# The first sequence's convolutions between the steps of the step-length preparation (layer 0 of a four-layer network)

## The chip, the cores and the metric

The kernel runs on one core of a Trainium2 chip. The metric is the time of one launch on the device, in microseconds (us), as the median of several runs; lower is better. One execution was taken with the hardware profiler. The engines are PE (matrix products), DVE (vector), ACT (scalar functions), POOL (general purpose), and SP, which issues most of the transfers. They run independently of each other, each takes its own instructions strictly in order, and they wait for each other through semaphores.

## The reference

Four layers work on four sequences of 512 tokens with 256 features, in float32. Each layer normalizes its input and adds the results of a mixer and of a feed-forward part, both from the same normalized input. The change concerns layer 0, whose mixer is a Mamba-2 state space model and whose feed-forward part is a gated unit:

```python
    x = L0_attn_hidden_states
    xn = _layernorm(x, axis=-1)
    x = x + _L0_attn_ref(xn, ...) + _L0_ffn_ref(xn, ...)
```

```python
            proj = jnp.einsum('bld,pd->blp', hidden_states, W_in)
            gate = proj[..., :INTER]
            hBC = proj[..., INTER:INTER + CONV_DIM]
            dt = proj[..., INTER + CONV_DIM:]
            xc = jnp.transpose(hBC, (0, 2, 1))
            conv = jax.lax.conv_general_dilated(xc, conv_w[:, None, :], ...)   # 4 taps, causal, per channel
            hBC = _silu(jnp.transpose(conv + conv_b[None, :, None], (0, 2, 1)))
            xs = hBC[..., :INTER].reshape(b, l, H, P)
            Bm = hBC[..., INTER:INTER + G * N].reshape(b, l, G, N)
            Cm = hBC[..., INTER + G * N:].reshape(b, l, G, N)
            ...
            dt = jax.nn.softplus(dt + dt_bias)
            A = -jnp.exp(A_log)
            dA = jnp.exp(dt * A)
            def step(h, inp):
                dA_t, dt_t, x_t, B_t, C_t = inp
                u = (dt_t[:, :, None] * x_t)[..., None] * B_t[:, :, None, :]
                h = dA_t[:, :, None, None] * h + u
                y = jnp.einsum('bhpn,bhn->bhp', h, C_t)
                return (h, y)
            ...
            g = y * _silu(gate)
            g = g * jax.lax.rsqrt(jnp.mean(g * g, axis=-1, keepdims=True) + EPS) * norm_w
            return jnp.einsum('bli,di->bld', g, W_out)
```

There are 32 heads of 64 channels (INTER = 2048), one group of B and C with 128 states, and 4 taps. So three things come out of the input projection: the channels x, B and C, which go through the convolution; the gate; and one step length per token and head, which doesn't. The step lengths dt decide how far each token's state decays.

## The kernel before, in words

Layer 0 runs as two interleaved streams, written as Python generators: `mamba_pieces` (the mixer) and `glu_units` (the gated feed-forward units, and also two sequences of a unit of layer 1). Each stream yields after a small piece of work and says with a number how much that piece is worth. `weave` always continues the stream that has done the smaller share of its announced total, 630.0 for the mixer and 207.0 for the gated units. The yielded numbers thus decide how many gated-unit pieces stand between two mixer pieces in the program. A scheduler then lays the instructions of each engine out in an order near that of the program; it may move an instruction ahead of one that isn't ready by its own reckoning, and it places the waits. It also assigns the buffers: tiles with one tag of one pool share a fixed number of buffers, and a new tile waits until the one before it in the buffer is no longer read. PSUM, where PE writes, has eight banks: four with the tag `mm`, two `tr` and two `acc`.

The mixer runs in this order:

- *The step lengths* (`with tc.tile_pool(name="m_pre", ...)`, lines 276 to 333): PE projects 32 numbers for each of the 2048 tokens into one bank (L142); DVE and ACT compute softplus from exp and a series of seven terms, about twenty DVE operations on 128x512 tiles (z, e, s, w, q; L285 to L305), into `dt`, and `dA`, the logarithm of the decay (L307). For each of the four sequences PE transposes dA (L315) and sums it along the chunk (L316); ACT exponentiates both into `row` tiles (L322), DVE sets the first decay of each chunk to zero (L324), and SP writes them to DRAM as `own` and `since` (L325). Two products (L331) and Exps (L332) give `after` and `etot`. All temporary tiles stand in a pool of their own, m_pre, which is closed behind this; only then are the pools of the rest opened. The piece yields 30, 20, 30, four times 1.5, and 2.
- *A sequence's B and C* (`sequence`): a projection (L134 on `ws`), the first tap on ACT (L264), three taps on DVE (L268) and Silu on ACT (L272) for each, and then transposes of B (L356) and products of B and C for the four chunks (L357, `CB`).
- *A group's channels* (`group(i, k)`, four tiles k for each of 16 groups i, a group being 512 channels, eight heads, of one sequence): projection, convolution to `xc`, and the gate's projection and Silu to `sg` (L388).
- *Chunks* of 128 tokens, 64 of them (16 groups of 4): SP loads the decays `G` from own, spread over 128 partitions (L394), and `eb` from since (L425); DVE turns G into running products with a scan (L409); PE transposes xc (L415), DVE multiplies by dt into `xdt`; POOL multiplies G by CB (L435); PE computes the part from the state (L456), the state's update (L464) and the part within the chunk (L474); y goes through the gate and into the output projection (L495), added on DVE (L501). The next group's tiles are computed within the chunks of the group before it.

The gated units' pieces are two projections (L134 on `wu`), Silu (L195), a product on DVE into `hT` (L196), and then the down projection (L203) with its addition into x (L151).

The first sequence and the first group have no chunk ahead of them to be computed in: `sequence(0)` and `group(0, 0..3)` stand between the step lengths and the first chunk.

Of the kernel before, what the change touches and what calls it, by code (L numbers as in the profile page):

```python
# [15 lines left out]
P = 128  # L16
# [3 lines left out]
TPB = SEQ // P  # L20
# [213 lines left out]
def mamba_pieces(c, a, ws, open_pool):  # L234
# [4 lines left out]
    nc, tc = c.nc, c.tc  # L239
    HG, HD = 8, 64  # L240
    by_head = lambda v: v[:, :, None].to_broadcast([P, HG, HD])
    keep = open_pool("m_keep", 1)
# [6 lines left out]
    wide = [P, NTILE, 32]  # L249
# [23 lines left out]

        return taps

    with tc.tile_pool(name="m_pre", bufs=1, side="right") as pool:

        pd = c.ps()
        for t in range(NTILE):
            project_tokens(  # L280
                c, pd[:, t * 32 : (t + 1) * 32], w_bcd, slice(256, 288),
                slice(t * P, (t + 1) * P),
            )
        z = c.tile(pool, wide, "z")
        nc.vector.tensor_add(z, v3(pd, 32), dt_bias[:, None, :].to_broadcast(wide))  # L285
        e = c.tile(pool, wide, "e")
        nc.vector.scalar_tensor_tensor(e, z, -1.0, z, ALU.mult, ALU.min)
        nc.scalar.activation(e, e, AF.Exp)
        expA = c.tile(pool, [P, 32], "expA")
        tc.keep_in_program_order(nc.scalar.activation(expA, a_log, AF.Exp))  # L290
        yield 30.0
        s = c.tile(pool, wide, "s")
        nc.vector.tensor_scalar_add(s, e, 2.0)
        nc.vector.reciprocal(s, s)
        nc.vector.tensor_mul(s, s, e)
        w = c.tile(pool, wide, "w")
        nc.vector.tensor_mul(w, s, s)
        q = c.tile(pool, wide, "q")
        nc.vector.tensor_scalar_mul(q, w, 1.0 / 17.0)
        yield 20.0  # L300
        for k in range(7, 0, -1):
            nc.vector.scalar_tensor_tensor(q, q, 1.0 / (2 * k + 1), w, ALU.add, ALU.mult)
        nc.vector.scalar_tensor_tensor(q, q, 1.0, s, ALU.add, ALU.mult)
        nc.vector.tensor_scalar_max(z, z, 0.0)
        nc.vector.scalar_tensor_tensor(dt, q, 2.0, z, ALU.mult, ALU.add)  # L305
        dA = c.tile(pool, wide, "dA")
        nc.vector.scalar_tensor_tensor(  # L307
            dA, dt, -1.0, expA[:, None, :].to_broadcast(wide), ALU.mult, ALU.mult
        )
        yield 30.0  # L310
        for b in range(NB):
            pa, pc = c.ps("tr"), c.ps("acc")
            for t in range(TPB):
                cols = slice(t * P, (t + 1) * P)
                nc.tensor.transpose(pa[:32, cols], dA[:, b * TPB + t, :], c.ident)  # L315
                nc.tensor.matmul(  # L316
                    pc[:32, cols], lhsT=dA[:, b * TPB + t, :], rhs=c.le, start=True, stop=True
                )
            tiles = slice(b * TPB, (b + 1) * TPB)
            for src, out in ((pa, own), (pc, since)):  # L320
                row = c.tile(pool, [32, TPB, P], "row", bufs=2)
                nc.scalar.activation(row, v3(src[:32, :], P), AF.Exp)  # L322
                if out is own:
                    nc.vector.memset(row[:, :, 0:1], 0.0)  # L324
                nc.sync.dma_start(out[tiles].rearrange("t h s -> h t s"), row)  # L325
            yield 1.5

        dAf = dA.rearrange("p t h -> p (t h)")
        for tri, out in ((c.gt, after), (c.ones, etot)):
            pc = c.ps()  # L330
            nc.tensor.matmul(pc, lhsT=tri, rhs=dAf, start=True, stop=True)  # L331
            nc.scalar.activation(out.rearrange("p t h -> p (t h)"), pc, AF.Exp)  # L332
        yield 2.0
# [4 lines left out]
    def load_in(i):  # L338
        w_in[i] = c.tile(pg2, [P, 2048], "w_in")
        nc.sync.dma_start(w_in[i], a["m_units"][i % 4][:, :2048])  # L340

    def sequence(b):

        tokens = slice(b * SEQ, (b + 1) * SEQ)
        BT = c.tile(pb, [P, SEQ], "BT", bufs=1)
        CT = c.tile(pb, [P, SEQ], "CT")
        for k, out in ((16, BT), (17, CT)):
            pc = c.ps()
            project(c, pc, w_bcd, slice((k - 16) * P, (k - 15) * P), tokens)
            taps = causal_conv(pool, pc, k, out)  # L350
            yield 1.7
            taps()
        pt, pcb = c.ps("tr"), c.ps("acc")
        for t in range(TPB):
            cols = slice(t * P, (t + 1) * P)
            nc.tensor.transpose(pt[:, cols], BT[:, cols], c.ident)  # L356
            nc.tensor.matmul(pcb[:, cols], lhsT=BT[:, cols], rhs=CT[:, cols], start=True, stop=True)  # L357
        Btok = c.tile(pb, [P, TPB, P], "Btok")
        CB = c.tile(pb, [P, TPB, P], "CB")
        nc.scalar.copy(Btok, v3(pt, P))  # L360
        nc.scalar.copy(CB, v3(pcb, P))
        acc = c.tile(pb, [P, TPB, DM], "acc")
        ssq = c.tile(pb, [P, TPB, 2, P], "ssq", bufs=1)
        seqs[b] = CT, Btok, CB, acc, ssq
        yield 1.3
# [25 lines left out]
    def decays(i, t):  # L391

        G = c.tile(pool, [P, HG, P], "G", bufs=3)
        nc.sync.dma_start(  # L394
            G.rearrange("p h t -> p (h t)"),
            own[i // 4 * TPB + t, i % 4 * HG : (i % 4 + 1) * HG, :]
            .rearrange("h t -> (h t)").partition_broadcast(P),
        )
        Gs[i, t] = G
# [90 lines left out]
    def project_out(i, t, y):  # L490
# [11 lines left out]
        if g == 3 and t == TPB - 1:  # L502
# [11 lines left out]
                add_scaled(c, b * TPB + u, acc[:, u, :], rs[:, u : u + 1])  # L514
            c.part_done(b)

    load_in(0)
    yield from sequence(0)
    for k in range(4):
        taps = group(0, k)  # L520
        yield 3.4
        taps()
    decays(0, 0)
    decays(0, 1)
    before(0, 0)
# [55 lines left out]
def layer0(c, a, x_in, con):  # L581

    with ExitStack() as stack:
        open_pool = lambda name, bufs, **kw: stack.enter_context(
            c.tc.tile_pool(name=name, bufs=bufs, **kw)
        )
        c.weights = open_pool("m_w", 1)
        unit = c.tile(c.weights, [P, 3072], "wu")
        ws = c.tile(open_pool("m_ws", 1), [P, 762], "ws")
        first_loads(c, a, x_in, con, ws, unit)  # L590
        for b in range(NB):
            layernorm(c, b)
            c.step(True)
        glu = open_pool("g0", 1)

        def glu_units():
            same = dict(bufs=5, out_tag="tr")
            yield from glu_pieces(c, glu, [unit], loaded=True, last=False, **same)
            yield from glu_pieces(c, glu, [a["g0_units"][1]], first=1, **same)

            yield from glu_pieces(
                c, glu, [a["g1_units"][0]], last=False, seqs=[0, 1], **same
            )

        c.parts(2, lambda b: layernorm(c, b, c.xn[b * SEQ : (b + 1) * SEQ, :]))
        weave(
            c,
            (mamba_pieces(c, a, ws, open_pool), 630.0, 0.0),
            (glu_units(), 207.0, 0.0),
        )  # L610

# [1169 lines left out]
```

## Time and profile before

| | us |
|---|---|
| median of three runs | 3194.76 (3190.83 to 3198.62) |
| time of the profiled execution | 3179.26 |
| its span | 3177.5 |
| PE busy in it | 3081.6 (97%) |
| DVE / ACT / POOL busy | 1851.9 / 1257.6 / 640.0 |

Layer 0 takes the first 830 us or so of the span; its last output product (L495) ends at 830.3. The tables list for each stage how long each engine was busy, how many of its instructions ran, the clock that PE was granted (1.00 is full) and the transfers. In lists in order of time a line gives the start, the busy time, engine, line, operation, what it writes and reads, how many instructions were merged into it, and in square brackets how long the engine was idle before it and what ended that. PE's matrix instructions appear twice, as the product and as the load of its stationary operand (PEld). One 512-column matmul instruction of the program appears as two in the trace.

### The profile page before, as it was taken

Reading aid. Unit: us, or ns where it says so; the run is one execution under the profiler, and the core shown is the slowest. Engines: PE = TensorE matmul, PEld = TensorE weight load, DVE = VectorE, ACT = ScalarE, POOL = GpSimd, SP = SyncE. Lnnn points to the kernel's source line nnn. Section 1 sums busy time; section 2 is a strip of 40 time slices with the busy share of each in tenths; the row PEclk is TensorE's granted clock in tenths of the full one; section 3 lists DMA queues with packets and bytes.
Section 4 is the critical chain, followed back from the end, with each engine's and each line's share of the span. In section 5 each row is a group of like instructions: output and inputs, shape, how many; then the busy total and the mean of one; then the engine's idle time right before and its main releaser. Section 6 shows DMA issues by size and latency. Waiting matters only on the chain.

```text
span 3177.5 us, 35877 instructions
## 1 busy us (share of the span) xinstructions
PE 3081.6 (97%) x12502; PEld 1879.8 (59%) x12502; DVE 1851.9 (58%) x4786; ACT 1257.6 (40%) x2908; POOL 640.0 (20%) x525
## 2 busy tenths in 40 slices
PE   8999999999899999999989999999999999999999
PEld 5566566565555555555566566566666665555555
DVE  5777778777677777887646654554554522222222
ACT  4434435444356666667424433333333401111111
POOL 0464545555400122331053000000000000000000
PEclk9999999999899999999999999999999999999999
DMA  4233233232310244344143000000000000000000
GB/s 130 77 103 119 93 95 110 89 117 83 110 36 25 68 98 116 103 112 142 47 113 110 7 21 7 1 27 1 21 1 1 20 20 20 20 20 20 0 0 27
DMA packets 89091, 185.16 MB, mean 58 GB/s; under 512 B 14192, under 2 KB 57216, under 8 KB 84176
## 3 DMA queue, kind: packets, MB, share of 16 engines
q1 hardware_dynamic: 74448, 135.05, 13.1%
q0 software_dynamic: 14176, 47.01, 6.1%
q8 instruction: 99, 1.62, 0.2%
q10 hardware_dynamic: 288, 0.82, 0.1%
q14 instruction: 80, 0.66, 0.1%
HBM read 160.95 MB, written 12.98 MB: 55 GB/s over the span
## 4 chain that ended last, share of the span: by engine, by line
PE 78%; DVE 10%; DMA 4%; POOL 3%; ACT 2%; issue 2%; SPq 1%; DVEq 0%; ACTq 0%; POOLq 0%
PE mm L134 31%; PE acc L203 8%; PE mm L631 7%; PE mm L142 5%; PE acc L1102 4%; PE acc L647 3%; DMA G<-own 2%; PE tr L1094 2%; PE tr L495 2%; DVE G L409 2%; DVE cy L268 2%; PE tr L812 2%; PE acc L856 1%; PE acc L869 1%; DMA psw<-pes 1%
## 5 line engine op out<-in xcount | busy, mean ns | idle before, releaser
L134 PE MATMUL mm<-xnT,wu 128*128 128x512 f32 x2128 | 955.6, 596 | 2.3 <-ACT sg L195 0.7
L134 PEld LDWEIGHTS mm<-xnT,wu 128*128 128x128 f32 x2128 | 398.4, 191 | 461.3 <-issue 430.8
L638 ACT ACTIVATE pr<-pr,nm 128x128 f32<-128x128 f32 (+3 forms) x512 | 285.9, 559 | 294.3 <-DVE nm L634 292.8
L195 ACT ACTIVATE sg<-mm 128x512 f32<-128x512 f32 x176 | 104.6, 594 | 607.0 <-PE mm L134 606.9
L196 DVE TENSOR_TENSOR hT<-sg,mm 128x512 f32<-128x512 f32 x176 | 120.4, 684 | 380.7 <-PE mm L134 369.0
L634 DVE CUSTOM_DVE_ANT_0 pr<-mm,late 128x128 f32<-128x128 f32 (+3 forms) x512 | 245.0, 482 | 88.3 <-PE mm L631 82.4
L203 PE MATMUL acc<-wu,hT 128*128 128x256 f32 x1280 | 290.9, 380 | 0.7 <-DVE x L151 0.4
L203 PEld LDWEIGHTS acc<-wu,hT 128*128 128x128 f32 x1280 | 240.0, 190 | 51.3 <-issue 19.2
L134 PE MATMUL mm<-xnT,w_in 128*128 128x512 f32 x512 | 231.1, 596 | 0.4 <-DVE hT L196 0.4
L973 POOL DMA_INDIRECT e<-in_p_experts,ids x128 | 128.4, 1003 | 451.7 <-DVE x L152 366.0
L409 DVE TENSOR_TENSOR_SCAN G<-G,eye 128x1024 f32<-128x1024 f32 x64 | 157.0, 2453 | 52.3 <-DMA G<-own 51.8
L631 PE MATMUL mm<-kf,qf 128*128 128x128 f32 (+3 forms) x512 | 179.1, 446 | 7.9 <-DVE qf L789 5.7
L435 POOL TENSOR_TENSOR G<-G,CB 128x1024 f32<-128x1024 f32 x64 | 151.8, 2372 | 162.0 <-DVE G L409 80.5
L268 DVE SCALAR_TENSOR_TENSOR cy<-mm,ws,cy 128x511 f32<-128x511 f32 (+2 forms) x216 | 158.7, 741 | 41.4 <-ACT cy L264 37.8
L631 PE MATMUL mm<-k,q 128*128 128x128 f32 (+3 forms) x512 | 176.6, 435 | 1.1 <-DVE q L1067 1.1
L421 ACT ACTIVATE xD<-xc,ws 128x128 f32<-128x128 f32 x256 | 84.8, 391 | 203.9 <-POOL y L458 191.6
L134 PEld LDWEIGHTS mm<-xnT,w_in 128*128 128x128 f32 x512 | 97.1, 192 | 101.3 <-issue 94.3
L152 DVE SCALAR_TENSOR_TENSOR x<-acc,cw,x 128x256 f32<-128x256 f32 x128 | 61.9, 483 | 155.5 <-PE acc L203 155.5
L1102 PE MATMUL acc<-PT,V 128*128 128x512 f32 (+3 forms) x512 | 149.5, 433 | 0.0
L1067 DVE TENSOR_SCALAR q<-mm,bias 128x512 f32<-128x512 f32 x64 | 48.0, 750 | 169.1 <-PE mm L134 169.1
L151 DVE TENSOR_TENSOR x<-acc,x 128x256 f32<-128x256 f32 x168 | 70.5, 421 | 118.4 <-PE acc L647 98.4
L812 PEld LDWEIGHTS tr<-con,pr 128*128 128x128 f32 x640 | 81.7, 143 | 90.2 <-ACT pr L805 28.8
(308 smaller groups left out, 5017.8 us busy)
## 6 DMA issues: line engine op xcount, KB each, us to landing
G<-own SPq DMA_DIRECT2D x64, 512.0 KB, 4.3
w_in<-in_m_units SPq DMA_DIRECT2D x16, 1024.0 KB, 5.2
eb<-since SPq DMA_DIRECT2D x96, 128.0 KB, 3.2
wu<-in_o_units SPq DMA_DIRECT2D x8, 1536.0 KB, 6.5
wo<-in_m_units SPq DMA_DIRECT2D x16, 512.0 KB, 3.8
psw<-pes SPq DMA_DIRECT2D x128, 64.0 KB, 2.6
wu<-in_g_units SPq DMA_DIRECT2D x4, 1536.0 KB, 6.8
wu<-in_f_units SPq DMA_DIRECT2D x4, 1536.0 KB, 6.9
```

Of the source, the lines that this page charges most:

```text
L134: c.nc.tensor.matmul(out, lhsT=w[:, d, cols], rhs=c.xnT[:, d, tokens], start=(d == 0), stop=(d == 1))
L142: c.nc.tensor.matmul(out, lhsT=c.xnT[:, d, tokens], rhs=w[:, d, cols], start=(d == 0), stop=(d == 1))
L203: nc.tensor.matmul(po, lhsT=hT[k][:, t * P : (t + 1) * P], rhs=wd[:, k, :], start=(i == 0), stop=(i == per - 1),)
L268: nc.vector.scalar_tensor_tensor(y[:, j:], src[:, : SEQ - j], conv[:, k, 3 - j : 4 - j], y[:, j:], ALU.mult, ALU.add,)
L409: nc.vector.tensor_tensor_scan(flat, flat, eye.rearrange("p h t -> p (h t)"), 0.0, ALU.mult, ALU.add)
L435: nc.gpsimd.tensor_mul(G, G, seqs[b][2][:, t, :][:, None, :].to_broadcast([P, HG, P]))
L631: nc.tensor.matmul(sc, lhsT=q[:, i * P : n], rhs=k[:, :n], start=True, stop=True)
L634: nc.vector.tensor_tensor_reduce(out=pr, in0=sc, in1=late[:, SEQ - n :], scale=1.0, scalar=-NEG, op0=ALU.add, op1=ALU.min, accum_out=nm,)
L638: nc.scalar.activation(pr, pr, AF.Exp, bias=nm, scale=-1.0, accum_out=total)
L812: nc.tensor.transpose(pt[:, (i - j) * P : (i - j + 1) * P], prs[s][i][:, j * P : (j + 1) * P], c.ident)
L973: nc.gpsimd.indirect_dma_start(out=e, out_offset=None, in_=a["p_experts"], in_offset=bass.IndirectOffsetOnAxis(ap=ids[:, t, k : k + 1], ax ...
L1102: nc.tensor.matmul(z[:, j * P :], lhsT=head["V"][:, j, h, :], rhs=head["PT"][:, j, j * P :], start=(j == 0), stop=(j == TPB - 1),)
```

## The change

The preparation of the step lengths becomes a generator, `time_steps`, like the other parts. Its tiles stand in the chunks' pool under the tags S, xw, eb and sq (two buffers each), which the chunks use later for other things; `expA` goes to the pool that stays, and the row tiles are the first 32 partitions of an sq tile. The pool m_pre is gone. The mixer now begins by loading the first group's weights and alternates: step lengths to e and its Exp; projection and first tap of B; the step lengths' s, w and the first q; the other taps of B and the projection of C; the rest of `sequence(0)`; the series, dt and dA; then the first tile of group 0; then the transposes, rows and products of dA; then the other three tiles. The pieces of the preparation yield 6, 4, 6, four times 1.5, and 2, and the mixer's announced total goes from 630 to 566.

```diff
-    with tc.tile_pool(name="m_pre", bufs=1, side="right") as pool:
+    def time_steps():
+
+        wide_tile = lambda tag: c.tile(pool, wide, tag)
...
-        z = c.tile(pool, wide, "z")
+        z, e = wide_tile("S"), wide_tile("S")
         nc.vector.tensor_add(z, v3(pd, 32), dt_bias[:, None, :].to_broadcast(wide))
-        e = c.tile(pool, wide, "e")
         nc.vector.scalar_tensor_tensor(e, z, -1.0, z, ALU.mult, ALU.min)
         nc.scalar.activation(e, e, AF.Exp)
-        expA = c.tile(pool, [P, 32], "expA")
+        expA = c.tile(keep, [P, 32], "expA")
         tc.keep_in_program_order(nc.scalar.activation(expA, a_log, AF.Exp))
-        yield 30.0
-        s = c.tile(pool, wide, "s")
+        yield 6.0
+        s, w, q = wide_tile("xw"), wide_tile("xw"), wide_tile("eb")
...
-        yield 20.0
+        yield 4.0
...
-        dA = c.tile(pool, wide, "dA")
+        dA = wide_tile("eb")
...
-        yield 30.0
+        yield 6.0
...
-                row = c.tile(pool, [32, TPB, P], "row", bufs=2)
+                row = c.tile(pool, [P, TPB, P], "sq")[:32]
...
     load_in(0)
-    yield from sequence(0)
+    steps, first = time_steps(), sequence(0)
+    for stream in (steps, first, steps, first, first, steps):
+        yield next(stream)
+    assert next(first, None) is None
     for k in range(4):
         taps = group(0, k)
         yield 3.4
         taps()
+        if k == 0:
+            yield from steps
...
-            (mamba_pieces(c, a, ws, open_pool), 630.0, 0.0),
+            (mamba_pieces(c, a, ws, open_pool), 566.0, 0.0),
             (glu_units(), 207.0, 0.0),
```

More of the change, by code (lines that the diff above doesn't have):

```diff
@@ L295, in mamba_pieces @@
         nc.vector.tensor_mul(s, s, e)
-        w = c.tile(pool, wide, "w")
         nc.vector.tensor_mul(w, s, s)
-        q = c.tile(pool, wide, "q")
         nc.vector.tensor_scalar_mul(q, w, 1.0 / 17.0)
-        yield 20.0
+        yield 4.0
         for k in range(7, 0, -1):
```

## The prediction

> **What bounds the kernel now.** I read the page's busy table first: PE is busy 3081.6 of 3177.5 us, so time is to be had only where PE waits or is slow. Then the table of stages for the part of layer 0 that the change can reach.
>
> ```profile
> PE 3081.6 (97%) x12502; PEld 1879.8 (59%) x12502; DVE 1851.9 (58%) x4786; ACT 1257.6 (40%) x2908; POOL 640.0 (20%) x525
> ...
> core 0: us, PE busy (x) PEld busy (x) DVE busy (x) ACT busy (x) POOL busy (x), PEclk, DMA share, GB/s
> 30.00:50.00 20.00, 20.00 (x65) 11.72 (x64) 16.92 (x25) 9.94 (x17) 0.00 (x0) 1.00 0.00 0
> 50.00:72.00 22.00, 21.31 (x79) 9.35 (x78) 1.83 (x7) 11.63 (x18) 0.00 (x0) 1.00 0.27 67
> 72.00:105.00 33.00, 29.02 (x91) 14.82 (x91) 27.07 (x32) 16.39 (x31) 8.37 (x5) 0.95 0.24 68
> 105.00:760.00 655.00, 637.94 (x3042) 396.20 (x3039) 512.23 (x661) 289.43 (x602) 349.12 (x236) 1.00 0.31 101
> ```
>
> PE is covered without a gap from 30 to 50 us, although DVE is then computing the step lengths: gate units fill it. DVE is idle from 50 to 72. From 72 to 105 PE loses about 4 us. In the 655 us behind it PE waits 17.1 us, at full clock. Next the order of time at the places that carry the sum:
>
> ```profile
> 30.18 0.69 DVE L285 TENSOR_TENSOR z<-mm,ws 128x512 f32<-128x512 f32 x1 [1.39 <-PE mm L142]
> ...
> 34.55 3.35 DVE L294 RECIPROCAL s<-s 128x512 f32<-128x512 f32 x1
> ...
> 48.10 0.69 DVE L307 SCALAR_TENSOR_TENSOR dA<-dt,expA 128x512 f32<-128x512 f32 x1
> ...
> 49.85 0.27 PE L315 MATMUL tr<-con,dA 128*32 128x128 f32 x1
> ...
> 85.47 4.02 DVE L409 TENSOR_TENSOR_SCAN G<-G,eye 128x1024 f32<-128x1024 f32 x1
> ...
> 91.63 0.33 PE L415 MATMUL tr<-con,xc 128*128 128x128 f32 x1 [2.26 <-ACT xc L272]
> ...
> 93.85 0.47 PE L415 MATMUL tr<-con,xc 128*128 128x128 f32 x1 [1.03 <-ACT xc L272]
> ...
> 104.64 1.09 PE L474 MATMUL acc<-G,xdt 128*64 128x128 f32 x16
> ```
>
> The step lengths are a DVE chain from 30.18 to 48.79. PE waits twice for a convolution's Silu, and behind these waits (94.1 to 97.2) its weight loads come 0.86 us apart instead of 0.43: half speed, 1.6 us lost. 104.64 is the first product with G of chunk 0; I use it as the milestone. Last, PE's waits from 105 to 760:
>
> ```profile
> PE tr L495 <- DVE x L151: 3.3, 3, 1.7
> ...
> PE tr L495 <- DVE acc L501: 2.3, 2, 2.0
> PE tr L356 <- ACT BT L272: 2.3, 2, 1.4
> ```
>
> They are short and scattered; only the third has one fixed place, the turn to a new sequence.
>
> **The change part by part.** Line numbers are those of before. No arithmetic is added or removed: the two built programs hold the same instructions on every engine. PE's order is the same from chunk 62 to the end, and that of the other engines from a little earlier or later, so only about 28 to 780 us can change.
>
> *Gate units leave the preparation.* In before, ahead of the milestone, PE's order holds 32 gate/up matmul instructions and 24 down matmuls (L134 on wu, L203); in after 16 and 12. A 512-column instruction takes 0.86 us (14 passes in 6.17 us), a down matmul 0.45 (16 passes in 3.62 us). So 16 x 0.86 + 12 x 0.45 = 19.2 us of PE work moves behind the milestone. After breaks even if it gets there at 104.64 - 19.2 = 85.4.
>
> *The chain of step lengths gets company on DVE.* Before, three hT products (0.69) and four adds into x (0.42) stood within it; after, three hT and six convolution taps (0.70 each). Its start is 29.4 instead of 30.18, as one gate matmul fewer stands ahead of the last projection. Sum from there: z, e, max 1.8; hT 2.1; the seven q steps 5.0; s and reciprocal 3.8; taps 4.2; s x e, w, q 1.8; last three 2.0; wait for ACT's Exp 0.3. That is 21.0, so dA is ready at 50.4, 1.6 later than before.
>
> *PE runs dry ahead of it.* After the projections end (29.3), PE's new order has eight 512-column tiles of 1.72 (BT's conv projection is done, CT's, two of group 0, five of gate units), four transposes 0.60 and CB 1.05 = 15.4 us, and then L315, which needs dA. So PE is out of work at 44.7 and waits until 50.4: 5.7 us, at a place where before had none. PE's queue is in order, so everything behind L315 waits too.
>
> *The clock behind that wait.* In before, 2.26 and 1.03 us of waiting were followed by 1.6 us lost at half speed, and a 3.72 us wait near the end of the layer (816 us) by rows 0.28, 0.89 and 0.50 longer than elsewhere, together 1.7. I take 1.7.
>
> The Trainium skill, "TensorE: Matmul & The Clock Gate", Part 1, has the clock fall after about 3.4 us of idleness; the 2.26 us wait above did it in this trace already, so the row decides. Its Part 4 says that transposes don't count as busy to the gate, which speaks against this change: the alternating transposes of L315 come right behind the wait. By that rule the 4.4 us of the first eight pairs would all run at half speed and the sum would be 2.7 us higher; the trace only shows that such pairs hold a full clock (50 to 54 us).
>
> *From dA to the milestone.* PE work in the new order: 12 alternating pairs of L315/L316 at 0.55 (their spacing from 50.39 on) = 6.6, the last four grouped 1.65, L331 2 x 0.94, ten 512-column tiles 17.2, twelve down matmuls 5.4, eight xc transposes 1.2, L464 0.95: 34.9. 50.5 + 1.7 + 34.9 = 87.1. Waits in between: the first scan of G (L409) sits on DVE ahead of the taps of group 0's second tile and must wait for its load. own is written at about 54.8, lands 1.7 later, G takes 4.7: DVE gets to the taps at about 65.4, when that tile's projection is only just done (63.6), so this costs PE little. The third scan meets POOL's product and takes 4.02 instead of 2.29, as in before's row; the Exps of the last sequence now stand on ACT, with two table loads of 1.28, between the tiles' Silus. By that walk xc of tiles 2 and 3 comes 1.0 and 1.4 us after PE asks for it: 2.4. Milestone 89.5, against 85.4: **+4.1**. That already counts the waits of before (about 4 us and 1.6) as gone.
>
> *What becomes free of the pool's end.* In before all tiles of the new pools wait for the closed pool: cy, G and others for the eight writes of row, the last issued at 65.90. In after SP issues the first G load behind one own write, and nothing waits for the rest. SP is otherwise waiting, so moving the eight writes among G, eb and w_in loads costs nothing while loads run a chunk ahead; if that cover went, a late G costs up to DVE's longest wait of 3.0. The borrowed buffers cost nothing: S, xw, eb and sq are first wanted by chunks at 82 or later, step lengths are done with them at about 60, the row writes at 76. POOL's queue keeps its order there.
>
> *The steady stage.* 19.2 us more gate work is spread over chunks 0 to 55 (3.15 us a chunk instead of 2.83). It is PE work either way and counted above; it helps only where it fills waits. At the turns to a new sequence PE had 4.3 us of work between CT's projection and the transposes of BT, and waited 1.35 and 0.93; after has 6.1 and 5.5 there: **-2.3**. For the other 14.8 us of waits, the count by 100 us (0.1, 3.4, 5.3, 2.0, 0.5, 4.2) doesn't follow the gate work in them, so I keep 14.8, plus 2.6% of the added 19.2: **+0.5**. Bounds: at the rate of the best window all would go (-14), at that of the worst (5.3 per 100 us) it would be 34 (+17).
>
> Sum: 4.1 - 2.3 + 0.5 = **+2.3 us**, on a profiled execution of 3179.26 (span 3177.5 and 1.8 around it). That run was 15.5 below the median of 3194.76; I add the difference to the median: **3197**.
>
> **The rivals.**
> 1. *More waits in the new order, slower.* One mechanism: DVE waits for a load of G (47.6 us in 32 waits between 105 and 760), the adds that empty PSUM queue behind the scan (L151, L501), and PE waits at L495, L203 or L415. The new order is a new draw, with more gate adds in DVE's queue. For: those releasers lead the list above. Against: 655 us at full clock hold only 17.1 us. It decides from 21 us of such waits (4 more). At a rate half way to the worst window, 26 us: 3197 + 9 = 3206; at the worst 3214, and a wait over 2 us brings another 1.7.
> 2. *The added filler takes the waits, faster.* For: -2.3 is visible; short chunks (4.5 us of PE work) are fewer. Against: windows rich in gate work waited as much. Half of the 14.8 gone: 3197 - 7.4 = 3190, with the first stage also 3 better 3187.
> 3. *The gap at 45 to 50 isn't there:* DVE gets through the chain with the taps in its own waits, and PE sees only the gain in the stage to 105. Against: DVE had only 1.3 us of waits in the chain. Then 5.7 + 1.7 go: 3190.
>
> **How the numbers follow.** A change under 0.2% (6.4 us) can't be told from none here. Forecast 0.38, spread about 4 us either way (0.02 faster, 0.30 within, 0.06 slower by more than 0.2%); rival 1 0.36 (0.34 slower); rival 2 0.20 (0.18 faster); rival 3 0.06 (0.02 faster). That makes faster 0.22, same 0.38, slower 0.40. The range reaches from rival 2 with half of its waits again (3184) to rival 1 at the worst window with three slow-clock stretches (3219). The forecast's own range is 3192 to 3202.
>
> **What would show it.** In the profile after: a PE wait of 4 to 7 us at the first L315, released by dA, near 45 to 50 us; half-clock spacing behind it; dA ending at 49.5 to 51.5; the milestone at 87 to 92; no wait at BT's transposes near two of the three turns; PE waits in the steady stage of 12 to 20 us. The forecast is wrong if the milestone comes before 85 or after 94, or if the steady stage's waits leave 9 to 25 us.

## The result and the profile after

The changed kernel is slower: 3201.1 us against 3191.02 us of the kernel before, medians of 17 runs each, a ratio of 1.0033 with a 95% interval of 1.0023 to 1.0042, that is 7 to 13 us. The profiled execution after took 3205.67 us (span 3203.9), the one before 3179.26. About half of these 26.4 us belong to the two executions and not to the change: in layers 1 to 3 all engines have the same instructions in the same order in both kernels, and yet the two executions differ there by about 14 us. The stages of layer 0 are therefore read one by one, each against its own beginning.

The busy table of after and its stages (per stage: length, busy time and instructions of PE, PEld, DVE, ACT and POOL, then PE's granted clock, DMA share, GB/s):

```profile
PE 3098.9 (97%) x12502; PEld 1890.4 (59%) x12502; DVE 1849.7 (58%) x4786; ACT 1257.4 (39%) x2908; POOL 635.9 (20%) x525
...
28.00:50.00 22.00, 17.47 (x62) 9.15 (x60) 19.98 (x29) 16.87 (x28) 0.00 (x0) 1.00 0.00 0
50.00:62.00 12.00, 11.44 (x38) 3.82 (x38) 1.63 (x4) 2.22 (x4) 0.00 (x0) 0.57 0.19 57
62.00:89.00 27.00, 27.00 (x92) 14.74 (x92) 18.89 (x25) 18.04 (x31) 10.08 (x5) 1.00 0.35 112
89.00:760.00 671.00, 647.50 (x3059) 403.43 (x3059) 505.63 (x655) 286.00 (x594) 330.30 (x231) 0.99 0.31 97
```

The instruction counts are those of before (12502, 4786, 2908, 525), but PE is busy 17.3 us longer in the whole span: the same products ran more slowly. In the first line PE lacks 4.5 of 22 us, where before had none. In the second it is busy and has a granted clock of 0.57. From 62 to 89 it is covered completely, where before waited. In the steady stage it waits 23.5 us.

The start and the first product with G of chunk 0, the milestone, in order of time. (The file is one line shorter here: before's L315 is L314, L474 is L473. The trace gives DVE's dA the buffer's tag, eb.)

```profile
30.36 0.69 DVE L287 TENSOR_TENSOR S<-mm,ws 128x512 f32<-128x512 f32 x1 [1.17 <-PE mm L142]
...
49.81 0.69 DVE L306 SCALAR_TENSOR_TENSOR eb<-dt,expA 128x512 f32<-128x512 f32 x1
...
50.56 0.40 PE L314 MATMUL tr<-con,eb 128*32 128x128 f32 x1 [5.09 <-DVE eb L306]
...
51.45 0.40 PE L314 MATMUL tr<-con,eb 128*32 128x128 f32 x1
...
57.70 2.08 PE L330 MATMUL mm<-eb,con 128*128 128x512 f32 x2
...
60.46 0.28 PE L314 MATMUL tr<-con,eb 128*32 128x128 f32 x1
61.01 0.28 PE L314 MATMUL tr<-con,eb 128*32 128x128 f32 x1
62.11 1.13 PE L330 MATMUL mm<-eb,con 128*128 128x512 f32 x2
...
88.88 1.09 PE L473 MATMUL acc<-G,xdt 128*64 128x128 f32 x16
```

The wait for dA is there, 5.09 us. Behind it the transposes come 0.89 us apart (50.56, 51.45); at 60.46 and 61.01 they come 0.55 apart. L330 takes 2.08 us before the clock is back and 1.13 after. So half clock lasted some 9.5 us and cost 8 x 0.34 (the first eight pairs) + 0.95 (L330) + 0.34 (one more pair) = 4.0 us.

The milestone is at 88.88. It was at 104.64, and 19.2 us of gate units have gone from ahead of it, so break-even was 85.4 and the loss is 3.4 us. Of this 1.0 us was there at the start: the normalization of the last sequence (L110), which stands before the change, began at 24.52 instead of 23.49. The first stage lost 2.4 us. In the row of the stage from 50 to 62 us the granted clock of 0.57 is the mean of half clock (0.50 from 50.5 to 59.5) and full clock behind it.

The steady stage is seen in one row of each kernel, all products with G (shortest, median and longest, then the first start and the last):

```profile
L473 PE MATMUL acc<-G,xdt x1024: 272/273/476, 88.9 to 837.3; 128*64 128x128 f32 x171
```

```profile
L474 PE MATMUL acc<-G,xdt x1024: 272/273/477, 104.6 to 824.6; 128*64 128x128 f32 x171
```

From the first to the last it is 748.4 us in after and 720.0 in before. Less the 19.2 us of moved gate work, after lost **9.2 us** on the way. PE's waits in it (released by; total, times, longest):

```profile
PE tr L203 <- DVE x L151: 5.3, 3, 2.3
PE tr L494 <- DVE y L479: 5.1, 1, 5.1
...
PE tr L355 <- ACT BT L272: 0.2, 1, 0.2
```

From chunk 0 to the last chunk PE waited 29.3 us instead of 24.5. This is 4.8 of the 9.2 us. The other 4.4 are PE's busy time, which grew by 23.6 us where 19.2 us of work came in: the products ran more slowly. The granted clock was 0.98 from 400 to 500, 0.97 from 600 to 700 and 0.97 from 700 to 760, where before had 1.00 in each; by these rounded figures that is 2 + 3 + 1.8 = 6.8 us. From 760 to 840 it was before that lost more (0.92 against 0.96), which takes some of this back.

One wait is new in kind, 5.05 us at 662. What led to it:

```profile
648.88 0.54 SPq L393 DMA_DIRECT2D G<-own  x1
...
653.36 2.29 DVE L408 TENSOR_TENSOR_SCAN G<-G,eye 128x1024 f32<-128x1024 f32 x1 [0.59 <-DMA G<-own]
...
655.79 2.35 POOL L434 TENSOR_TENSOR G<-G,CB 128x1024 f32<-128x1024 f32 x1 [2.83 <-DVE G L408]
656.15 0.68 DVE L456 TENSOR_TENSOR y<-acc,eb 128x512 f32<-128x512 f32 x1
...
659.10 1.27 POOL L457 TENSOR_TENSOR y<-y,xD 128x512 f32<-128x512 f32 x1
660.40 0.69 DVE L478 TENSOR_TENSOR y<-acc,y 128x512 f32<-128x512 f32 x1 [3.57 <-POOL y L457]
661.34 0.68 DVE L479 TENSOR_TENSOR y<-y,sg 128x512 f32<-128x512 f32 x1
662.08 2.93 PE L494 MATMUL tr<-wo,y 128*128 128x256 f32 x6 [5.05 <-DVE y L479]
```

SP issues the load of G when a buffer is free; DVE waits for its data at the scan, here only 0.59 us. The first step of y (L456) stands behind the scan in DVE's queue and starts at 656.15. By then POOL has begun the product of G, and behind that xw, the state update's operand (L437, 1.05 us from 658.10), so y's next step (L457) comes at 659.10, and PE gets y at 662.08. PE, for its part, asks for this y (chunk 47, counted from 0) at 657.03, 3.5 us after the chunk's products with G began (L473 at 653.57): only the output products of the chunk before (L494) and four transposes stand between. With L494 2.93 us instead of 1.56 behind the wait and L134 5.17 instead of 3.70, at a granted clock of 0.50 from 662 to 668, this one place cost 5.05 + 1.4 + 1.5 = 7.9 us, most of the 9.2 (7.0 in the second profile of after, reported below).

In before, 19.0 us lie between the same two instructions of chunk 47, with projections and gate units in them. And little cover alone does no harm: for chunk 45 PE asks after 4.2 us and doesn't wait. There y's first step starts 0.20 us after its product on PE, with no scan ahead of it:

```profile
633.50 0.69 DVE L457 TENSOR_TENSOR y<-acc,eb 128x512 f32<-128x512 f32 x1 [0.20 <-PE acc L456]
634.25 1.09 PE L474 MATMUL acc<-G,xdt 128*64 128x128 f32 x16
638.43 0.60 PE L495 MATMUL tr<-wo,y 128*128 128x256 f32 x2
...
650.53 1.09 PE L474 MATMUL acc<-G,xdt 128*64 128x128 f32 x16
...
669.54 1.99 PE L495 MATMUL tr<-wo,y 128*128 128x256 f32 x8
```

### The profile page after: what moved, and what is told of

It is laid out like the page before. It is cut to its first block, busy times and chain, and to the rows that moved or that the text cites. A ratio compares the mean times of both kernels' runs of the same rounds, so it can differ in the third digit from the quotient of the medians.

```text
span 3203.9 us, 35866 instructions
## 1 busy us (share of the span) xinstructions
PE 3098.9 (97%) x12502; PEld 1890.4 (59%) x12502; DVE 1849.7 (58%) x4786; ACT 1257.4 (39%) x2908; POOL 635.9 (20%) x525
## 4 chain that ended last, share of the span: by engine, by line
PE 78%; DVE 10%; DMA 4%; POOL 3%; ACT 3%; issue 2%; SPq 1%; DVEq 0%; ACTq 0%; POOLq 0%
PE mm L134 30%; PE acc L203 8%; PE mm L636 7%; PE mm L142 5%; PE acc L1107 4%; PE acc L652 3%; DMA G<-own 2%; PE tr L1099 2%; PE tr L494 2%; PE tr L817 2%; DVE G L408 2%; DVE cy L268 2%; PE acc L874 1%; PE acc L861 1%; DMA psw<-pes 1%
## 5 line engine op out<-in xcount | busy, mean ns | idle before, releaser
L134 PE MATMUL mm<-xnT,wu 128*128 128x512 f32 x2128 | 958.3, 597 | 2.4 <-DMA wu<-in_g_units 2.3
L134 PEld LDWEIGHTS mm<-xnT,wu 128*128 128x128 f32 x2128 | 401.0, 191 | 463.2 <-issue 437.9
L203 PE MATMUL acc<-wu,hT 128*128 128x256 f32 x1280 | 290.9, 380 | 0.4 <-DVE x L151 0.2
L203 PEld LDWEIGHTS acc<-wu,hT 128*128 128x128 f32 x1280 | 240.0, 190 | 51.0 <-issue 19.2
L134 PE MATMUL mm<-xnT,w_in 128*128 128x512 f32 x512 | 231.1, 594 | 2.2 <-DVE cy L268 1.9
L134 PEld LDWEIGHTS mm<-xnT,w_in 128*128 128x128 f32 x512 | 96.0, 190 | 108.2 <-issue 95.8
L494 PE MATMUL tr<-wo,y 128*128 128x256 f32 x512 | 129.5, 396 | 7.9 <-DVE y L479 5.1
```

The costliest lines, as they stand in the source:

```text
L134: c.nc.tensor.matmul(out, lhsT=w[:, d, cols], rhs=c.xnT[:, d, tokens], start=(d == 0), stop=(d == 1))
L203: nc.tensor.matmul(po, lhsT=hT[k][:, t * P : (t + 1) * P], rhs=wd[:, k, :], start=(i == 0), stop=(i == per - 1),)
L494: nc.tensor.matmul(po, lhsT=y[:, k, :], rhs=groups[i][1][:, k, :], start=(k == 0), stop=(k == 3))
```

## The experiments

The change has two halves that can be made alone: the interleaving (with the borrowed buffers), and the smaller yields, which take gate units away. My theory after the result was that the first stage's loss is the gap that the missing gate units leave, with the clock behind it, and that the steady loss comes with the new places of the gate units. Its rivals were that the interleaving itself costs, that the steady loss is chance of one execution, or that it is a fault in POOL's order. In the table, "first" is the way from the start to the milestone and "way" that from chunk 0 to the last chunk. Both are gains (-) or losses (+) in us against before's profiled execution, with moved gate work taken off, and come from the one profiled execution of each kernel. The ratio is to the kernel before on the same chip.

| kernel | yields; total | ratio (95%) | PE gap at dA | first | way |
|---|---|---|---|---|---|
| before, second look | 30/20/30; 630 | one run | none | +1.4 | +1.4 |
| after, again | 6/4/6; 566 | 1.0044 (1.0029 to 1.0058) | 5.08 | +2.0 | +8.9 |
| interleaving alone | 30/20/30; 630 | 0.9966 (0.9952 to 0.9981) | none | -6.4 | +5.4 |
| yields alone | 6/4/6; 566 | 1.0085 (1.0062 to 1.0108) | 14.50 | +18.3 | +11.6 |
| after, gap filled | 6/4/6; 566 | 1.0028 (1.0015 to 1.0042) | dummy products | +1.1 | +16.0 |
| after, POOL's order kept | 6/4/6; 566 | 1.0026 (1.0011 to 1.0041) | 5.08 | +2.4 | +14.7 |
| after, 576 | 6/4/6; 576 | 1.0000 (0.9988 to 1.0013) | 5.08 | +2.7 | -3.3 |
| half | 12/8/24; 594 | 1.0026 (1.0013 to 1.0038) | 2.37 | -0.4 | +4.2 |
| 20 | 20/12/20; 602 | 0.9955 (0.9937 to 0.9974) | none | -5.9 | -2.2 |
| 20, again | 20/12/20; 602 | 0.9958 (0.9945 to 0.9970) | none | -5.9 | -3.9 |
| 24 | 24/16/24; 614 | 0.9995 (0.9982 to 1.0008) | none | -5.5 | +2.5 |
| interleaving alone, POOL's order kept | 30/20/30; 630 | 0.9989 (0.9977 to 1.0001) | none | -7.8 | +8.2 |

"First" repeats within about 1.5 us. "Way" of a single execution can be several us off: "interleaving alone" adds to -1.0 in its profiled execution and is 10.9 us faster by its runs (0.0034 of 3209.86). The profiled execution of "after, gap filled" (3230.75) was the longest of its twelve runs (median 3218.96), so its way of +16.0 says little.

**The same two kernels again.** No edit.

> The changed kernel once more, for a second profile. Read so far from one profile of each: at the first L473 (chunk 0) the changed kernel stands 3.5 us behind before once the 19.2 us of moved gate work is taken off, at chunk 8 5.5, at chunk 40 7, and behind one wait of PE of 5.05 us (662 us, L494 on y) 16; at the last chunk 13. Theory (the order of the instructions sets these waits): the second profile shows the same curve within 2 us at chunk 0 and 3 us behind it, with the large wait between chunks 47 and 48 again; ratio to before 1.003. Rival (chance of the one execution, such as late loads of G): the curve from chunk 8 on differs by 5 us or more and the wait at 662 us is gone, while the median stays 10 us above before.

> The kernel before once more, for a second profile to hold the others against. Theory (the waits follow from the order of the instructions): the waits of PE at 71 to 94 us (4.7 in sum, half clock behind them) and the one of 2.6 us near 382 come again; the way from chunk 0 to chunk 63 is within 3 us of the 719.2 us of the first profile. Rival (chance of one execution): it differs by 5 us or more, and then the 9 us that the changed kernel loses on that way are in doubt.

After's second profile has the gap (5.08 us), a first stage of +2.0 and a way of +8.9, and the wait for y of chunk 47 again (5.01 us at 661.70). Before's second look has its waits of 2.26 and 1.04 us ahead of chunk 0 and a way within 1.4 us of its first. Two profiles of each kernel thus agree within 1.5 us, and both losses belong to the order of the instructions and not to the chance of one execution.

**Each half alone.** On after, and the opposite on before (6.0, 4.0, 6.0 and 566.0):

```diff
-        yield 6.0
+        yield 30.0
...
-        yield 4.0
+        yield 20.0
...
-        yield 6.0
+        yield 30.0
...
-            (mamba_pieces(c, a, ws, open_pool), 566.0, 0.0),
+            (mamba_pieces(c, a, ws, open_pool), 630.0, 0.0),
```

> The interleaving and the borrowed buffers of the change, but with the yields 30, 20, 30 and the total 630 of before, so that as many gate units stand in the preparation as before (38.3 us of PE work ahead of chunk 0), and the same PE order as before from chunk 0 on. Theory (the slowdown comes from the gate units that left the preparation: PE's gap of 5.1 us, 4.0 us at half clock behind it, and about 7 us of waits in the order of the later chunks that goes with the other numbers): no gap ahead of L314, full clock, and before's waits at 91 and 94 us (3.3, and 1.6 at half clock) are smaller; chunk 0 1 to 5 us earlier than in before, the rest as before: 3186 to 3191 beside 3191, ratio 0.998 to 1.000. Rival A (the interleaving itself is what costs, through the longer DVE chain): slower than before by 3 us or more, with dA 3 us or more later than in before and PE waiting for it.

> The opposite half: the order of before without any interleaving, with a pool of its own, but with the yields 6, 4, 6 and the total 566 of the change. The order of PE from chunk 0 on is that of the changed kernel. Theory: PE has neither gate units nor convolutions ahead of L315, runs out at about 33 us and waits for dA until about 47: 14 us, 4 us at half clock behind it, and the waits for the first group's convolutions stay (about 5): chunk 0 is 16 to 20 us behind before with the moved gate work taken off, the later chunks add what they add in the changed kernel (2 to 12): 3209 to 3223, ratio 1.006 to 1.010. Rival A (the interleaving costs, the numbers don't matter): within 3 us of before.

The interleaving alone is faster, 0.9966; I had expected only 0.998 to 1.000, as the first stage gained 6.4 us and not 1 to 5. Its order of time at dA:

```profile
57.94 3.60 PE L134 MATMUL mm<-xnT,w_in 128*128 128x512 f32 x8
61.37 0.27 PE L314 MATMUL tr<-con,eb 128*32 128x128 f32 x1
...
61.91 0.28 PE L314 MATMUL tr<-con,eb 128*32 128x128 f32 x1
```

PE has projections until it takes up dA; the same transposes run at full speed, 0.54 apart, and no wait stands ahead of them. The yields alone are the slowest kernel of all:

```profile
47.43 0.37 PE L315 MATMUL tr<-con,dA 128*32 128x128 f32 x1 [14.50 <-DVE dA L307]
...
48.29 0.40 PE L315 MATMUL tr<-con,dA 128*32 128x128 f32 x1
...
58.12 2.08 PE L331 MATMUL mm<-dA,con 128*128 128x512 f32 x2
```

Without projections of the first sequence and with few gate units PE waits 14.50 us for dA, and the pairs come 0.86 apart. From the four ratios on this chip: interleaving is worth 0.9966 - 1 = -0.0034 with the large yields and 1.0044 - 1.0085 = -0.0041 with the small ones, -11 and -13 us. The small yields cost 1.0044 - 0.9966 = 0.0078 and 0.0085, 25 and 27 us. Within the intervals the two halves add up: -0.0034 + 0.0085 = 0.0051, against 1.0044 for both. The kernel with the yields alone also has the 5-us wait at L495 for y (5.12 us at 680.74); the interleaving has no part in it.

**The gap without the clock.** Six products whose result nothing uses are put ahead of the transposes of dA in after, so that PE doesn't go idle:

```diff
+        hot = c.ps("acc")
+        for _ in range(6):
+            tc.keep_in_program_order(nc.tensor.matmul(
+                hot, lhsT=c.xnT[:, 0, :P], rhs=c.xnT[:, 0, :SEQ], start=True, stop=True
+            ))
         yield 6.0
         for b in range(NB):
```

> The changed kernel with six 512-column matmuls of xnT by xnT into a PSUM bank that nothing reads, placed ahead of the last gate tile in front of the gap (6 x 0.86 = 5.2 us): the gap's length in work without use; the order behind is the changed kernel's own. Theory (4.0 us are lost at half speed behind the gap, because PE stood still): the pairs of L319/L320 come 0.55 apart instead of 0.89, chunk 0 3 to 4.5 us earlier than in the changed kernel, ratio 0.9985 to 0.999 to it. Rival (the pairs run slowly by themselves, for want of work or for what their operands' places cost, not by the clock): spacing still 0.85 to 0.9, time as the changed kernel or up to 0.5 us longer.

The products fill 48.73 to 54.05 (this execution began 5.5 us later than before's). All lines here are five higher than in after:

```profile
48.73 5.32 PE L311 MATMUL acc<-xnT 128*128 128x512 f32 x12
...
55.60 0.27 PE L319 MATMUL tr<-con,eb 128*32 128x128 f32 x1
...
56.14 0.28 PE L319 MATMUL tr<-con,eb 128*32 128x128 f32 x1
59.99 1.12 PE L335 MATMUL mm<-eb,con 128*128 128x512 f32 x2
```

The same transposes, with nothing idle ahead of them, are 0.54 apart and the last product takes 1.12 instead of 2.08. That the pairs were slow in after was thus an effect of the wait ahead of them. What came of it is less than expected: the first stage is +1.1 instead of +2.0 to 2.4. The dummies made PE take up dA 1.06 us after it was there, and a wait of 1.68 us (81.54) that had been hidden now shows: 2.7 of the 4.0 us. The ratios, 1.0028 and 1.0044, point the same way, but their intervals overlap.

**POOL's order.** At 655.79 POOL does the product of G and y's addition comes behind it. I took this for the cause of the 5-us wait, and kept both in the program's order:

```diff
-        nc.gpsimd.tensor_mul(G, G, seqs[b][2][:, t, :][:, None, :].to_broadcast([P, HG, P]))
+        tc.keep_in_program_order(nc.gpsimd.tensor_mul(
+            G, G, seqs[b][2][:, t, :][:, None, :].to_broadcast([P, HG, P])
+        ))
...
-            nc.gpsimd.tensor_add(y, y, xD)
+            tc.keep_in_program_order(nc.gpsimd.tensor_add(y, y, xD))
```

> The changed kernel with POOL's addition into y (L457) and its product of G by CB (L434) kept in the order of the program on POOL, so that y of a chunk never stands behind the product of a later chunk; PE's order is the changed kernel's, instruction by instruction. In the changed kernel y of chunk 47 stands on POOL behind the product of chunk 49 and xw of chunk 48, which wait for a late G, and PE stands still for 5 us at 662, then runs slowly. Theory: that wait shrinks to under 2 us and the jump between chunks 47 and 48 from 9 us to under 3; in sum 3 to 8 us faster than the changed kernel unless the products, now later, make L473 wait elsewhere; ratio to before 1.001 to 1.003. Rival (the wait comes from the load of G or from DVE, POOL's order is no matter): the wait stays at 4 us or more, time as the changed kernel.

> The interleaving with the yields and total of before, and POOL's y and G kept in program order as well: PE's order is that of the full filling. Theory: chunk 0 as with the full filling (6 us ahead of before); in the later chunks y comes earlier and the products later: where PE waits for x or acc behind a late y (about 8 us in sum in before) some of it goes; ratio 0.995 to 0.997. Rival (POOL's order is right as it is, the products are then late): L473 waits for POOL, ratio 0.997 to 1.000.

The theory fell. In after with POOL's order kept:

```profile
665.69 2.85 DVE L408 TENSOR_TENSOR_SCAN G<-G,eye 128x1024 f32<-128x1024 f32 x1 [0.90 <-DMA G<-own]
669.04 0.67 DVE L458 TENSOR_TENSOR y<-acc,eb 128x512 f32<-128x512 f32 x1
670.20 1.26 POOL L459 TENSOR_TENSOR y<-y,xD 128x512 f32<-128x512 f32 x1
671.42 2.35 POOL L434 TENSOR_TENSOR G<-G,CB 128x1024 f32<-128x1024 f32 x1
672.43 1.88 DVE L481 TENSOR_TENSOR y<-y,sg 128x512 f32<-128x512 f32 x1
674.37 2.49 PE L496 MATMUL tr<-wo,y 128*128 128x256 f32 x6 [4.54 <-DVE y L481]
```

POOL now adds y first (670.20), and PE still waits 4.54 us, again for chunk 47 and again asking 3.8 us after its products began (665.99). What remains is the head of the chain: the scan, 2.85 us long and 0.90 us late for G, and y behind it. Part of what POOL gave was taken again, since DVE's product with the gate (L481) now runs beside POOL's product and takes 1.88 us instead of 0.68. On the interleaving alone the same edit gained nothing: 0.9989 against 0.9966 on the other chip, intervals that just overlap, and the products with G (L475) then wait for POOL, 1.48 and 0.72 us. Another order on POOL alone thus doesn't remove the loss.

**Between the two, and the total alone.** Other yields with their totals on after, as in the table; the last edit is only this:

```diff
-            (mamba_pieces(c, a, ws, open_pool), 566.0, 0.0),
+            (mamba_pieces(c, a, ws, open_pool), 576.0, 0.0),
```

> The change with the yields 20, 12, 20 and the total 602, between the full filling (30, 20, 30, 630) and the change (6, 4, 6, 566): 31.3 us of gate work ahead of chunk 0 instead of 38.3 or 19.2; later chunks in an order of their own. Theory (the gate units that leave the preparation cost their gap only where PE runs dry): PE doesn't run dry ahead of L314 or by less than 1 us, chunk 0 4 to 7 us ahead of before with the moved work taken off; the later chunks are a new order and may lose 0 to 8 us: ratio 0.997 to 1.000. Rival (each microsecond that leaves the preparation costs about the same, 25 us for 19.1): 9 us slower than the full filling, ratio 0.999 to 1.000 with chunk 0 not ahead of before.

> The yields 20, 12, 20 with the total 602 once more, beside its neighbours on one chip. Theory: ratio to before 0.994 to 0.997 again, chunk 0 about 6 us ahead of before with the moved work taken off, the way from chunk 0 to 63 not longer than in before by more than 3 us. Rival (its 0.9955 was a favourable session): 0.997 to 1.000.

> The yields 12, 8, 24 with the total 594: 27.8 us of gate work ahead of chunk 0, of which less stands early in the preparation than with 20, 12, 20. Theory: PE runs dry ahead of L314 by 0 to 2 us (10.5 us of the 19.1 moved back covers a gap of 5.1), chunk 0 2 to 6 us ahead of before; the later order is a new one, 0 to 9 us: ratio 0.997 to 1.001. Rival (a straight line in the gate work that stays): 0.9966 + 10.5/19.1 x 0.0070 = 1.000 to 1.001, with chunk 0 1 to 2 us behind before.

> The yields 24, 16, 24 with the total 614: 34.7 us of gate work ahead of chunk 0. Theory: the first stage is that of the neighbours, 5 to 7 us ahead of before, no gap ahead of L314; a new order behind it, 0 to 6 us: ratio 0.995 to 0.999. Rival (a straight line between 0.9966 and 1.0036): 0.9975 to 0.9985.

> The changed kernel with the mixer's announced total 576 instead of 566, nothing else: as much gate work leaves the preparation (19.2 us ahead of chunk 0), but the gate units stand in other places among the later chunks. Theory (the loss behind chunk 0 belongs to where the gate units fall, above all to chunks left with 6 us of PE work): chunk 0 about 2 us behind before as in the changed kernel; the wait of 5 us of L494 between chunks 47 and 48 is gone or elsewhere, and the loss from chunk 0 to 63 differs from 9 us by 3 or more, in either direction: ratio 0.999 to 1.005, not 1.0036 within 0.0006. Rival (the loss belongs to the amount moved into the later chunks, wherever it falls): 8 to 12 us again, ratio 1.003 to 1.0045.

With a total of 576 the first stage is that of after (gap 5.08 us, +2.7), and yet the kernel is as fast as before, 1.0000. PE's longest waits from 87 to 760 us:

```profile
PE tr L203 <- DVE x L151: 3.0, 2, 1.9
PE tr L494 <- DVE acc L500: 2.9, 2, 2.0
```

The wait of 5 us is gone, none is over 2.0 up to 760 us, and the way is -3.3 instead of +9 (1.8 us of that because four down matmuls now stand behind the last chunk). The same work with the gate units a little further apart is thus some 10 us faster. The steady loss of the change is a matter of where the gate units fall; it doesn't follow their amount. Nor does it follow how late the loads of G are: over the whole span DVE waits for them at the scan 51.8 us in before, 51.0 in after, 58.5 here, and 34.2 in after with POOL's order kept, whose 1.0026 can't be told from after's time.

The half-sized yields show the same from the other side. There the gap is only 2.37 us and the first stage even with before. Half clock still followed it for some 10 us of transposes and products (0.50 from 54 to 62 us; L203 usually takes 1.89):

```profile
52.76 0.28 PE L314 MATMUL tr<-con,eb 128*32 128x128 f32 x1 [2.37 <-DVE eb L306]
...
61.42 2.97 PE L203 MATMUL tr<-wu,hT 128*128 128x256 f32 x8
```

And the order of chunks has a 5-us wait elsewhere, of the same making (scan, POOL's product and xw ahead of y):

```profile
311.48 2.29 DVE L408 TENSOR_TENSOR_SCAN G<-G,eye 128x1024 f32<-128x1024 f32 x1 [3.15 <-DMA G<-own]
...
320.10 1.19 PE L494 MATMUL tr<-wo,y 128*128 128x256 f32 x2 [5.04 <-ACT xD L420]
```

The profile names ACT as what ended the wait; y's last step on DVE (L479, 319.26 to 319.95) ended 0.1 us before. I had expected 0.997 to 1.001 of it and got 1.0026: between the two ends the time doesn't fall steadily with the yields. The largest of the set, 24/16/24 with 614, has the better first stage too (-5.5), but an order of chunks that gives it back, and at 0.9995 just misses the 0.995 to 0.999 that I expected. The yields 20/12/20 with 602 are the best kernel of the study, 0.9955 (where I had expected 0.997 to 1.000) and again 0.9958, about 14 us below before. Its stages in the second of the two:

```profile
28.00:50.00 22.00, 22.00 (x85) 13.77 (x84) 18.98 (x28) 12.72 (x22) 0.00 (x0) 1.00 0.00 0
50.00:72.00 22.00, 22.00 (x84) 10.24 (x83) 9.81 (x16) 11.63 (x20) 2.37 (x1) 1.00 0.33 93
72.00:92.00 20.00, 19.24 (x56) 8.57 (x56) 14.84 (x19) 12.79 (x22) 7.83 (x4) 1.00 0.25 83
92.00:760.00 668.00, 653.75 (x3105) 407.32 (x3100) 524.77 (x670) 295.40 (x612) 358.49 (x239) 1.00 0.32 100
```

PE is covered up to 72 us, loses 0.8 before chunk 0 and waits 14.3 us in the steady stage, all at full clock. The gain has two sources: 5.9 us ahead of chunk 0, twice, mostly because PE's waits for the convolutions (about 4 us in before) and the half clock behind them (1.6) are gone; and the way, 2 to 4 us shorter than in before's profile. The second is near the spread of a single profile.

**Not tried.** No run starts the load of G earlier (G has three buffers), and none moves only y's first step ahead of the scan on DVE. So the chain behind the 5-us waits is read from the traces and wasn't tested by taking it apart. In the three shown the late load itself is 0.59, 0.90 and 3.15 us; the rest is the scan, what POOL does ahead of y, and PE asking early.

## Why the time lay in the range, and what was wrong in the ground

The time of 3201.1 lies in the range, and in the forecast's own range of 3192 to 3202 too. That flatters it: the forecast stood on a median before of 3194.76, and 17 runs give 3191.02. The forecast was a change of +2.3 us; the measured one is +10.1, on the side to which I gave the largest chance (slower, 0.40), but mostly through waits in the new order, which I had left to a rival. In the profile the change is +2.4 in the first stage and +9.2 behind it, together 11.6; the prediction had +4.1 and -1.8.

- **PE runs dry ahead of dA.** Right. Predicted: dA at 50.4, a wait of 5.7. Measured: 50.50 and 5.09.
- **The clock behind that wait.** Right in kind, mis-sized: 1.7 predicted, 4.0 measured. The 1.7 came from two places where the clock was back after 3 to 4 us (94.1 to 97.2, and 817 to 821); here half clock lasted 9.5 us over short transposes. At 662, behind a wait of the same length but with longer products, it lasted 6 us (4 in the second profile). The Trainium skill, "TensorE: Matmul & The Clock Gate", Part 4, says that a transpose doesn't count as busy to the gate in the same way; by that the prediction named 4.4 us lost in the first eight pairs. The total of 4.0 lies near this by luck: these eight pairs lost 2.7 of it, and the rest came behind them. That they stayed slow fits the page. But the runs with no wait ahead show these transposes at full clock, so at most it can hold for how the clock comes back, not for how it is kept.
- **From dA to the milestone.** Mis-sized: 2.4 us of waits for the convolutions of tiles 2 and 3 were predicted, none came (27.00 of 27.00 us busy from 62 to 89). The slow PE asked for them later; when the dummies kept the clock up, 1.68 us of such waiting appeared. The two misses nearly cancel: milestone 89.5 predicted, 88.88 measured; stage +4.1 against +3.4, or +2.4 without the later start.
- **Waits at the turns, -2.3.** Half right: 0.2 us is left at BT's transposes, but at the same three turns PE now waits 1.0 us for C (L356 for CT), so 1.1 is gained.
- **The rest of the steady waits, +0.5.** This is the step that failed. Taking the other 14.8 us over unchanged assumed that a reshuffle of the gate units is neutral. It cost 9 us, 4.8 of them waits and the rest slower products behind them; up to 760 us PE waited 23.5 us, outside of the 12 to 20 that I gave, though inside the 9 to 25 beyond which I called the forecast wrong. What happened is near the first rival's mechanism (what stands behind the scan is late, PE waits), at another place than I named: y's first step rather than the adds that empty PSUM, and PE at L494 for y. Its first link, DVE waiting for G, was the smaller part: 0.59 us at the wait that mattered, and no more in sum than in before. Its price, 3206 against 3197, was +9.
- **The second and third rivals.** The gap was there. That the added filler would take waits away held in part for the turns and for nothing else in this order. With a total of 576 the way was 3.3 us shorter than before's, but by one profile and with the 1.8 us named above.
- **What I didn't look for.** The change was priced as one thing. Its two halves pull apart, -11 to -13 and +25 to +27 us, and a set of yields between them beats both kernels. The 5.7 us gap against "PE is covered from 30 to 50 by gate units" already pointed there.

## What to carry to other kernels

When work is moved so that an engine's gap closes by itself, keep the filler that covered the gap until the trace shows that it isn't needed: here interleaving gained 11 to 13 us and cutting the filler in the same edit cost 25 to 27. A wait of several us on PE costs more than its length, so price the half clock behind it by the work that follows: here 5.09 us with short transposes behind it cost another 4.0, and 5.05 us with products of 256 and 512 columns another 2.9 (2.0 in the second profile). Before moving filler, look at what each engine's queue puts ahead of the value that the bottleneck will ask for next. Where a weave of two streams sets the order, one number in its shares can be worth 10 us with no work changed; try a few neighbours, with runs enough to tell 0.2%, before judging any restructuring by one of them.

## What the runs showed of the hardware that I had not expected

- Behind a wait of 5.09 us PE stayed at half clock for some 9.5 us of alternating transposes and small products; behind 14.50 us it lasted longer still (L331 at 58.12, 10.7 us after PE had restarted, took 2.08, and the granted clock was 0.50 up to 62 us). Behind a wait of only 2.37 us with the same transposes behind it (yields 12/8/24) it was some 10 us, behind 5.05 us with longer products 4 to 6. With no idle time ahead of them the same pairs ran at full clock for as long as they lasted.
- DVE's two-input product on 128x512 (y times the gate) took 1.88 us instead of 0.68 when POOL's product on 128x1024 ran beside it, so putting POOL's work earlier can take from DVE what it gives to POOL. Not every DVE product suffers: y's first step, which reads one input from PSUM, took 0.68 beside the same POOL product (656.15 in after).
- Two executions of identical instruction orders (layers 1 to 3) differed by about 14 us, with the granted clock at 0.98 for 400 us in one of them (2400 to 2800, 1.00 in the other) and 0.96 against 0.98 from 840 to 1200. Differences under some 10 us between two single profiles are best read stage by stage.
